# VectorE's background operations of a scan step, issued between the scan and its product

## The chip, the cores and the metric

The kernel runs on one core of a Trainium2 chip. The metric is the device time of one execution in microseconds. A core has five engines that run their own instruction queues in order: TensorE (PE in the profile; PEld is its weight loads), VectorE (DVE), ScalarE (ACT), GpSimd (POOL) and SyncE (SP, which issues the DMAs here). They wait for each other through semaphores.

## The reference

Eight images of 64 x 64 x 96 pass through two residual layers. The first, which fills nearly all of the time, is a two-dimensional state space layer: group norm, an input projection, a depthwise 3 x 3 convolution with SiLU, then a scan over the 4096 pixels in four directions, a layer norm, a gate and an output projection. The second is a group norm followed by an MLP on a twice upsampled image. The scan, for each of 4 directions, 192 channels and 16 states:

```python
def step(h, inp):
    ul, dl, Bl, Cl = inp
    dA = jnp.exp(dl[..., None] * A)
    h = dA * h + (dl * ul)[..., None] * Bl[:, :, None, :]
    y = jnp.einsum('bkdn,bkn->bkd', h, Cl)
    return (h, y)
```

## The kernel before

The 128 partitions of a scan tile are 8 channels by 16 states; its free dimension is a chunk of 1024 pixels. An image takes 4 directions x 4 chunks x 24 tiles, so 8 images make 3072 tiles, one step of the main loop each (`for i in range(n + 4)`). All instructions are issued in an order written out by hand; each engine runs its own in that order. For a tile there are:

- `fetch` (L1063), six steps ahead: a DMA that broadcasts delta * u (`du`) to the tile `dub`.
- `product_b` (L1069), three steps ahead: GpSimd multiplies `dub` by `br` into `bb`, one of four buffers.
- `decay` (L1075, L1082), one step ahead: four TensorE matmuls spread delta over the partitions into `pd` in PSUM, which has two buffers, and ScalarE takes the exponential in place.
- `scan` (L1089): VectorE's scan along the chunk, from `pd` and `bb`, started from the tile's column of `carry`. In steps with `i % 3 == 2` (`by_pool`) it writes to a tile `h` of its own, in the others back into `pd`.
- `product_c` (L1095): the product of the states by C (`cr`) into `hc`, on VectorE; for a `by_pool` tile on GpSimd, in the next step.
- `hold` (L1108): the last column of the states is copied to `carry`, on VectorE, for a `by_pool` tile on ScalarE. The last chunk of a direction has none.
- `sums` (L1127): TensorE adds `hc` over the states into `py`, for two tiles in every other step.

The scan's `pd` is thus read by the product and by the copy of the carry, in two of three steps, and the same buffer is written by the decay of the tile two steps later.

All else, that is the norms, projections, convolutions, gates and the MLP of other images and the deltas of the next chunk, is background work. It is written as generators that `Side` keeps in lists. One call of `side.advance` in each step lets the generators issue their next pieces, within caps on what a step may take of each engine. VectorE's pieces are few: `dl` (L1028), the convolution's and the gate's product (L585, L628), the statistics (L471, L481) and the layer norm's two products (L719, L720). The other engines' pieces are issued by the same call. A piece usually comes a step after the pieces of other engines that it reads. After `side.advance`, `turn_over` puts in a filler matmul (L1101) where the step had little for TensorE.

Of the kernel before, what the change touches and what calls it, by code (L numbers as in the profile page):

```python
# [136 lines left out]
def kernel(ctx: ExitStack, tc: tile.TileContext, a: dict, out: bass.AP):  # L137
# [133 lines left out]
    def constants_in():  # L271
        nc.gpsimd.memset(xp, 0.0)
        raw["sel"] = tile_([128, 8, 128], "sel_0")
        for hf in range(2):
            nc.sync.dma_start(
                raw["sel"][64 * hf : 64 * hf + 64].rearrange("p j m -> p (j m)"),
                a["sel_b"][0:64, 0:2].rearrange("r q j m -> r (q j m)"),
            )
        raw["dt_b"] = tile_([C, K, HF], "dt_b")
        nc.sync.dma_start(raw["dt_b"], a["dt_b"])  # L280
        names = ("xp_dt", "xp_c", "xp_b")
        raw["xp"] = [tile_([128, K, Q3, R if n == "xp_dt" else NS], n) for n in names]
        ds = raw["ds"] = tile_([128, Q3, K], "ds")
        for hf in range(2):
            for q, r0, r1, f, c0 in pieces:
                rows, src = slice(64 * hf + r0, 64 * hf + r1), slice(c0, c0 + r1 - r0)
                for t, name in zip(raw["xp"], names):
                    nc.sync.dma_start(t[rows, :, q, :], a[name][src, :, f, 0 : t.shape[-1]])
                nc.sync.dma_start(ds[rows, q, :], a["ds"][src, f, :])
        for name, shape in (("coef", [128, 3, 3]), ("w2", [128, 3, C]), ("b2", [128, C])):  # L290
            raw[name] = tile_(shape, name)
            nc.sync.dma_start(raw[name], a[name])
# [766 lines left out]
    def fetch(t):  # L1059
        assert t["got"]["ready"]  # L1060
        t["dub"] = sp.tile([128, T], F32, tag="dub", name="dub", bufs=4)
        g = t["g"]
        nc.sync.dma_start(  # L1063
            t["dub"], t["got"]["du"][None, 8 * g : 8 * g + 8, :].to_broadcast([NS, 8, T])
        )

    def product_b(t):
        t["bb"] = sp.tile([128, T], F32, tag="bb", name="bb", bufs=4)
        nc.gpsimd.tensor_tensor(t["bb"], t["dub"], t["got"]["br"], ALU.mult)  # L1069

    def decay(t):
        pd = t["pd"] = psd.tile([128, T], F32, tag="pd", name="pd")
        for hf in range(2):
            rows = slice(64 * hf, 64 * hf + 64)
            nc.tensor.matmul(  # L1075
                pd[:, MB * hf : MB * hf + MB],
                sel_b[rows, 4 * t["s"] + t["j"]].rearrange("p n c -> p (n c)"),
                t["got"]["dl"][rows, t["q"], :],
                start=True,
                stop=True,  # L1080
            )
        nc.scalar.activation(pd, pd, AF.Exp, scale=neg_a[:, t["k"], t["g"] : t["g"] + 1])  # L1082
# [10 lines left out]
    def product_c(t):  # L1093
        t["hc"] = sp.tile([128, T], F32, tag="hc", name="hc", bufs=4)
        (nc.gpsimd if t["by_pool"] else nc.vector).tensor_tensor(t["hc"], t["h"], t["got"]["cr"], ALU.mult)  # L1095

    def turn_over():

        if side.spent < 1.0 and side.free:
            n, p = side.bank("idle")  # L1100
            nc.tensor.matmul(p, ident, sel_b[:, 0:4].rearrange("p j n c -> p (j n c)"), start=True, stop=True)  # L1101
            side.give(n)

    def hold(t):
        if t["last"]:
            return
        end = T - 1 if t["k"] < 2 else 0
        (nc.scalar.copy if t["by_pool"] else nc.vector.tensor_copy)(  # L1108
            carry[:, t["g"] : t["g"] + 1], t["h"][:, end : end + 1]
        )  # L1110
# [61 lines left out]
    with tc.manual_schedule():  # L1172
        side.queue = [bp.open("setup")]
        side.drain()
        constants_in()
        start, rest = front(0)
        side.queue = start[:-4]
        side.drain()
        side.queue = start[-4:] + [(8, 0, constants_of_scans), (8, 0, constants_of_mlp)]
        side.drain()  # L1180
        side.urgent = prepare(0, tiles[0]["k"], tiles[0]["i0"], tiles[0]["got"])
        side.queue, rest = rest[:4], rest[4:]
        while side.urgent or side.hurried:
            side.advance({e: (2 * most, 2 * most) for e, (_, most) in Side.CAPS.items()}, 2, 0)
        n = len(tiles)
        for i in range(FETCH):
            fetch(tiles[i])
            if i >= FETCH - LEAD:
                product_b(tiles[i - FETCH + LEAD])
        decay(tiles[0])  # L1190
        begin, *side.later = prepare(0, tiles[NT]["k"], tiles[NT]["i0"], tiles[NT]["got"])
        total = 1
        for i in range(n + 4):
            t = tiles[i] if i < n else None
            at = i % (NT * NCH * K)
            if t and t["i"] == 0:
                b = t["b"]
                if at == 0:
                    y_dram[b] = [dr.tile([DI, L], F32, tag=f"y{o}", name=f"y{o}") for o in range(2)]
                    side.begun, hasty = 0, sum(item[1] for item in rest) if b == 0 else 0  # L1200
                    side.queue += rest
                    down, end = [], []
                    if b:
                        keep = {}
                        side.queue += tail(b - 1, keep)
                        up, down, end = mlp(b - 1, keep)
                        side.queue += up
                    if b + 1 < images:
                        start, rest = front(b + 1)
                        side.queue += start[:2] + [i for two in zip(down, start[2:10]) for i in two] if b else start[:10]  # L1210
                        side.queue += start[10:] + rest
                        rest = []
                    else:
                        side.queue += down
                    side.queue += end
                    total = sum(item[1] for item in side.queue)
                if b == images - 1 and at == NT * NCH * (K - 1):
                    keep = {}
                    side.queue += tail(b, keep, pairs=False)
                    total = 0  # L1220

            ahead = 4 if i < 2 * NT else 8
            if (i + ahead) % NT == 0 and i + ahead + NT < n:
                nxt = tiles[i + ahead + NT]
                begin, *side.later = prepare(nxt["b"], nxt["k"], nxt["i0"], nxt["got"])
                side.urgent.append(begin)

            if i == 2:
                side.urgent.append(begin)
            if i == 4 or i and i % NT == 0:  # L1230
                side.urgent += side.later
                side.later = []
            if t and t["i"] % 8 == 4:
                before(t)
            if i + FETCH < n:
                fetch(tiles[i + FETCH])
            if 0 < i <= n and tiles[i - 1]["by_pool"]:
                product_c(tiles[i - 1])
            if i + LEAD < n:
                product_b(tiles[i + LEAD])  # L1240
            if i + 1 < n:
                decay(tiles[i + 1])
            if t:
                scan(t)
                if not t["by_pool"]:
                    product_c(t)
                hold(t)
            ends = i % 2 == 1 and 3 <= i <= n + 2
            adds = ends and tiles[i - 2]["j"] == 3 and tiles[i - 2]["k"]
            side.advance(  # L1250
                Side.CAPS,
                2 if not total or side.begun < max(hasty, total * at / 290) else 0,
                0 if 7 <= i % NT <= 21 else 1,
                0.95 * (bool(ends) + bool(adds)),
            )
            turn_over()
            if ends:
                sums(tiles[i - 3 : i - 1])
                if tiles[i - 2]["j"] == 3:
                    side.stores.append([g := store(tiles[i - 2]), next(g)])  # L1260
        up, down, end = mlp(images - 1, keep)
        side.queue += up + down + end
        side.drain()
# [89 lines left out]
```

## Time and profile before

| | |
|---|---|
| median of 3 runs | 11111.8 us (11110.65 to 11118.07) |
| profiled execution, first to last instruction (its span) | 11105.8 us |
| the same execution's other time | none recorded; the span is 6.0 us under the median |
| VectorE busy, instructions | 10207.5 us, 7702 |
| GpSimd busy | 10179.6 us |
| TensorE busy | 9967.9 us, 932.0 of it filler (L1101) |
| ScalarE busy | 5910.6 us |
| mean granted TensorE clock | 0.982 |
| one scan on VectorE | 2.28 to 2.35 us, 3072 of them |
| one product on VectorE | 1225 ns, 2048 of them |
| one copy of the carry on VectorE | 148 ns, 1536 of them |

The busy shares tell how full an engine is over the whole span, not which engine sets the end. The list of waits has the waiting engine and line, the releaser, the time in total, the number of waits and the longest. A wait for several semaphores is put down to the one that came last. A row of the timeline has the start and the duration in us, engine, line, operation, the tiles (out<-in) and shapes, and in brackets the idle time of the engine before it with its releaser.

### The profile page before, as it was taken

Reading aid. Unit: us, or ns where it says so; the run is one execution under the profiler, and the core shown is the slowest. Engines: PE = TensorE matmul, PEld = TensorE weight load, DVE = VectorE, ACT = ScalarE, POOL = GpSimd, SP = SyncE. Lnnn points to the kernel's source line nnn. Section 1 sums busy time; section 2 is a strip of 40 time slices with the busy share of each in tenths; the row PEclk is TensorE's granted clock in tenths of the full one; section 3 lists DMA queues with packets and bytes.
Section 4 is the critical chain, followed back from the end, with each engine's and each line's share of the span. In section 5 each row is a group of like instructions: output and inputs, shape, how many; then the busy total and the mean of one; then the engine's idle time right before and its main releaser. Section 6 shows DMA issues by size and latency. Waiting matters only on the chain. (4 is left out here: it accounts for less than half of the span.)

```text
span 11105.8 us, 137238 instructions
## 1 busy us (share of the span) xinstructions
PE 9967.9 (90%) x45020; PEld 3204.6 (29%) x45020; DVE 10207.5 (92%) x7702; ACT 5910.6 (53%) x8218; POOL 10179.6 (92%) x4674
## 2 busy tenths in 40 slices
PE   8898888989889998999889998899988989889988
PEld 2222222322233222332223322233222332223325
DVE  6999999999999999999999999999999999999990
ACT  5455445656455564555545555455554655545543
POOL 5999999999999999999999999999999999999990
PEclk9999999999999999999999999999999999999998
DMA  6888898898988989888988989889898898988981
GB/s 174 215 208 224 209 231 209 217 227 232 233 209 216 225 231 225 212 218 224 240 217 215 224 221 244 209 219 225 217 243 210 217 228 218 247 206 216 227 214 48
DMA packets 1044463, 2401.27 MB, mean 216 GB/s; under 512 B 293820, under 2 KB 314556, under 8 KB 1043752
## 3 DMA queue, kind: packets, MB, share of 16 engines
q1 hardware_dynamic: 1042776, 2391.45, 86.5%
q8 instruction: 361, 5.91, 0.2%
q14 instruction: 350, 2.87, 0.1%
q10 hardware_dynamic: 976, 1.04, 0.0%
HBM read 1929.05 MB, written 328.73 MB: 203 GB/s over the span
## 5 line engine op out<-in xcount | busy, mean ns | idle before, releaser
L1069 POOL TENSOR_TENSOR bb<-dub,br 128x1024 f32<-128x1024 f32 x3072 | 7173.5, 2359 | 208.4 <-DMA dub<-du 149.2
L1082 ACT ACTIVATE pd<-pd,neg_a 128x1024 f32<-128x1024 f32 x3072 | 3340.7, 1088 | 4533.0 <-PE pd L1075 4489.8
L1075 PE MATMUL pd<-dl,sel_b 64*128 64x512 f32 x12288 | 3512.7, 645 | 987.2 <-DVE carry L1108 649.2
L1089 DVE TENSOR_TENSOR_SCAN pd<-pd,carry,bb 128x1024 f32<-128x1024 f32 x1536 | 3610.3, 2350 | 262.2 <-ACT carry L1108 127.9
L1095 POOL TENSOR_TENSOR hc<-h,cr 128x1024 f32<-128x1024 f32 x1024 | 2413.9, 2357 | 352.6 <-DVE h L1089 300.7
L1095 DVE TENSOR_TENSOR hc<-pd,cr 128x1024 f32<-128x1024 f32 x2048 | 2508.4, 1225 | 164.1 <-PE py L1127 20.0
L1075 PEld LDWEIGHTS pd<-dl,sel_b 64*128 64x128 f32 x12288 | 966.7, 186 | 3266.3 <-issue 1511.2
L1089 DVE TENSOR_TENSOR_SCAN h<-pd,carry,bb 128x1024 f32<-128x1024 f32 x768 | 1797.3, 2340 | 5.8 <-ACT pd L1082 5.6
L1127 PE MATMUL py<-hc,sel_r 128*32 128x512 f32 x12288 | 1715.0, 617 | 30.4 <-POOL hc L1095 30.2
L1089 DVE TENSOR_TENSOR_SCAN pd<-pd,bb 128x1024 f32<-128x1024 f32 x512 | 1172.5, 2290 | 98.6 <-ACT carry L1108 75.3
L1101 PE MATMUL idle<-sel_b,ident 128*128 128x512 f32 x1652 | 932.0, 646 | 8.0 <-DVE ty L720 5.9
L562 PE MATMUL pc<-pad,convr 96*128 96x512 f32 (+1 forms) x2304 | 858.3, 616 | 5.7 <-DVE e L585 3.6
L1089 DVE TENSOR_TENSOR_SCAN h<-pd,bb 128x1024 f32<-128x1024 f32 x256 | 583.6, 2280 | 26.0 <-ACT pd L1082 25.2
L1127 PEld LDWEIGHTS py<-hc,sel_r 128*32 128x32 f32 x12288 | 250.3, 109 | 1109.0 <-issue 854.5
L1031 POOL TENSOR_TENSOR u<-dl,u 128x512 f32<-128x512 f32 x384 | 485.0, 1271 | 79.2 <-DVE dl L1028 79.2
L862 PEld LDWEIGHTS p<-w2q,mq 128*100 128x100 f32 x4800 | 452.9, 168 | 274.6 <-issue 214.2
L855 PE MATMUL ph<-xu,w 96*128 96x500 f32 x960 | 504.9, 629 | 11.5 <-ACT mq L856 6.7
L862 PE MATMUL p<-w2q,mq 128*100 128x96 f32 x4800 | 511.5, 258 | 2.3 <-ACT mq L856 2.3
L562 PEld LDWEIGHTS pc<-pad,convr 96*128 96x128 f32 (+1 forms) x2304 | 266.3, 163 | 563.9 <-issue 552.8
L987 PE MATMUL px<-u,xp 64*64 64x512 f32 x1536 | 422.4, 627 | 2.4 <-issue 2.4
L1101 PEld LDWEIGHTS idle<-sel_b,ident 128*128 128x128 f32 x1652 | 249.8, 189 | 596.5 <-issue 522.4
L1012 PE MATMUL pv<-xd,dt_w 64*64 64x512 f32 x1536 | 394.4, 609 | 1.0 <-ACT xd L997 1.0
(153 smaller groups left out, 6707.9 us busy)
## 6 DMA issues: line engine op xcount, KB each, us to landing
dub<-du SPq DMA_DIRECT2D x3072, 512.0 KB
u<-u SPq DMA_DIRECT2D x256, 384.0 KB
du<-u SPq DMA_DIRECT2D x768, 128.0 KB
y<-yq SPq DMA_DIRECT2D x768, 128.0 KB
br<-xd SPq DMA_DIRECT2D x256, 256.0 KB
cr<-xd SPq DMA_DIRECT2D x256, 256.0 KB
yp<-y SPq DMA_DIRECT2D x384, 128.0 KB
yp<-u SPq DMA_DIRECT2D x192, 128.0 KB
```

The source lines that it names most:

```text
L562: nc.tensor.matmul(t[rows].rearrange("p (i j) -> p i j", i=8), weights[:, cs], v["pad"][:, 8 * blk + kw : 8 * blk + kw + 8, kh : kh + H], ...
L855: nc.tensor.matmul(t[:, :px], w1[:, m, :], xu, start=True, stop=True)
L862: nc.tensor.matmul(t[:SIDE, C * i : C * i + C], sq[:, m, row], w2q[:, m, :], start=(m == 0), stop=(m == 2))
L987: nc.tensor.matmul(p[rows], xp[rows, k, q, :], v["u"][rows, q, :], start=(q == 0), stop=(q == 2), skip_group_check=True,)
L1031: nc.gpsimd.tensor_tensor(v["u"][:, q, :], got["dl"][:, q, :], v["u"][:, q, :], ALU.mult)
L1069: nc.gpsimd.tensor_tensor(t["bb"], t["dub"], t["got"]["br"], ALU.mult)
L1075: nc.tensor.matmul(pd[:, MB * hf : MB * hf + MB], sel_b[rows, 4 * t["s"] + t["j"]].rearrange("p n c -> p (n c)"), t["got"]["dl"][rows, t[" ...
L1082: nc.scalar.activation(pd, pd, AF.Exp, scale=neg_a[:, t["k"], t["g"] : t["g"] + 1])
L1089: nc.vector.tensor_tensor_scan(t["h"][:, ::step], pd[:, ::step], t["bb"][:, ::step], 0.0 if t["first"] else held, ALU.mult, ALU.add)
L1095: (nc.gpsimd if t["by_pool"] else nc.vector).tensor_tensor(t["hc"], t["h"], t["got"]["cr"], ALU.mult)
L1101: nc.tensor.matmul(p, ident, sel_b[:, 0:4].rearrange("p j n c -> p (j n c)"), start=True, stop=True)
L1127: nc.tensor.matmul(py[r0 : r0 + 32], sel_r[:, t["j"], :], t["hc"][:, MB * hf : MB * hf + MB], start=(t["j"] == 0), stop=(t["j"] == 3 and t ...
```

## The change

In the steps whose product is VectorE's, the product by C and the copy of the carry are issued after the call of `side.advance` instead of ahead of it. VectorE's order in such a step was scan, product, copy, background; it becomes scan, background, product, copy. In the `by_pool` steps the order stays: scan, ScalarE's copy, background.

```diff
             if t:
                 scan(t)
-                if not t["by_pool"]:
-                    product_c(t)
-                hold(t)
+                if t["by_pool"]:
+                    hold(t)
             ends = i % 2 == 1 and 3 <= i <= n + 2
             adds = ends and tiles[i - 2]["j"] == 3 and tiles[i - 2]["k"]
             side.advance(
...
                 0.95 * (bool(ends) + bool(adds)),
             )
+            if t and not t["by_pool"]:
+                product_c(t)
+                hold(t)
             turn_over()
             if ends:
                 sums(tiles[i - 3 : i - 1])
```

## Prediction

> **What bounds the kernel now.** I read the busy shares first, then who waits for whom on VectorE, then single rows in order of time.
>
> From the profile page, part 1:
>
> ```profile
> PE 9967.9 (90%) x45020; PEld 3204.6 (29%) x45020; DVE 10207.5 (92%) x7702; ACT 5910.6 (53%) x8218; POOL 10179.6 (92%) x4674
> ```
>
> Three engines stand at 90% or more. The busy time by stretches says that the scans run from 120 to 10835 us; in these 10715 us VectorE is busy for 10162 us and GpSimd for 10150 us, 95% each. Which of them leads is told by the waits. VectorE's waits, the longest three:
>
> ```profile
> DVE pd L1089 <- ACT carry L1108: 203.2, 414, 3.6
> DVE pd L1089 <- ACT pd L1082: 113.8, 238, 8.0
> DVE pd L1089 <- POOL bb L1069: 40.2, 38, 2.3
> ```
>
> VectorE's scan waits for ScalarE (the exponential of the decay, or the copy queued beside it: 317 us) and hardly for GpSimd (40 us). GpSimd in turn waits 301 us for VectorE's `h`. So VectorE leads, and the wait that ends last in front of its scans is the decay's.
>
> Steps go in threes. I call them A, B (product on VectorE) and C (`by_pool`, product on GpSimd). Going through the trace's 3072 scans in order, the idle time in front of A's scan is 324 us, of B's 37, of C's 32. A group of three, from the timeline (only its VectorE, decay and exponential rows):
>
> ```profile
> 3351.92 2.35 DVE L1089 TENSOR_TENSOR_SCAN pd<-pd,carry,bb 128x1024 f32<-128x1024 f32 x1
> ...
> 3354.37 1.23 DVE L1095 TENSOR_TENSOR hc<-pd,cr 128x1024 f32<-128x1024 f32 x1
> 3355.51 0.15 DVE L1108 COPY carry<-pd 128x1 f32<-128x1 f32 x1
> 3355.57 2.34 DVE L1089 TENSOR_TENSOR_SCAN h<-pd,carry,bb 128x1024 f32<-128x1024 f32 x1
> 3355.77 0.33 PEld L1075 LDWEIGHTS pd<-dl,sel_b 64*128 64x128 f32 x4 [1.41 <-PE ph L855]
> 3355.80 1.13 PE L1075 MATMUL pd<-dl,sel_b 64*128 64x512 f32 x4 [0.63 <-DVE carry L1108]
> 3356.97 1.09 ACT L1082 ACTIVATE pd<-pd,neg_a 128x1024 f32<-128x1024 f32 x1 [1.08 <-PE pd L1075]
> 3358.16 2.36 DVE L1089 TENSOR_TENSOR_SCAN pd<-pd,carry,bb 128x1024 f32<-128x1024 f32 x1 [0.25 <-ACT carry L1108]
> ```
>
> Rows one to three are step B, row four is C, the last is the next A. There are two `pd` buffers, so A's decay may start only when B's copy of the carry, the last reader of that buffer, is over (3355.66). From there: 0.11 to the weight load and 1.16 to the matmuls' end, 0.04 to the exponential, 1.09 in it, 0.10 to the scan: 2.50 us. Beside it VectorE has only C's scan, over at 3357.91, so it idles 0.25. Next to a scan that waits for nothing (which starts 0.08 before its forerunner's recorded end) this is 0.33 us lost.
>
> The same place where step B has a background operation (VectorE alone):
>
> ```profile
> 2806.43 1.23 DVE L1095 TENSOR_TENSOR hc<-pd,cr 128x1024 f32<-128x1024 f32 x1
> 2807.57 0.15 DVE L1108 COPY carry<-pd 128x1 f32<-128x1 f32 x1
> 2807.63 0.68 DVE L1028 SCALAR_TENSOR_TENSOR dl<-pv,e 128x512 f32<-128x512 f32 x1
> 2808.23 2.28 DVE L1089 TENSOR_TENSOR_SCAN h<-pd,bb 128x1024 f32<-128x1024 f32 x1
> 2810.43 2.27 DVE L1089 TENSOR_TENSOR_SCAN pd<-pd,bb 128x1024 f32<-128x1024 f32 x1
> ```
>
> Here `dl` fills the time and A's scan follows without idling.
>
> **What the change moves.** Only two VectorE instructions of steps A and B, the product and the copy of the carry, go behind `side.advance`. Neither issues a DMA, and no order changes on TensorE, ScalarE, GpSimd or SP; what changes there is when their waits on VectorE end. Nothing happens in a step without background work. By count over the trace, such work stands in 190 A steps, 222 B steps and 294 C steps; C keeps its order.
>
> **Gain: the distance between scan and product.** Over 2048 pairs the product starts 0.080 us after the scan's end on average (half at 0.035, half at 0.105; above, 3351.92 + 2.35 = 3354.27, then 3354.37). Pairs in which the second doesn't read what the first wrote overlap by 0.084 (product to copy, copy to background, background to scan). One background pair that does depend, L719 to L720, is 0.035 apart as well. So the distance belongs to the dependence. With a background operation between, both distances become -0.084: 0.164 us saved per step, 412 x 0.164 = 67.6 us.
>
> [...]
>
> **Cost 1: the decay of the next A.** In B the copy of the carry now follows the background work, so the 2.50 us begin 0.60 - 0.16 = 0.43 later (a lone operation of 0.68 takes 0.60 with its overlap), and the cover is C's scan alone. In 66 of the 222 groups C has background work too; it takes 0.6 or more, over the 0.33 needed: nothing is lost. In the other 156, 119 did not wait before and now lose 0.33 each: 39.3 us. By hand: -67.6 + 39.3 = -28.
>
> **Cost 2: where TensorE is behind anyway.** In a quarter of the groups with work in B the decay's weight load came 0.5 us or more after the copy: TensorE was busy with background matmuls, A's scan waited for it, and VectorE's gain vanishes in that wait. So I took group by group the later of two times, VectorE free (0.164 earlier per moved step) and the exponential's end (later by what the copy is later), carrying a late copy of A through TensorE's idle time to the next A. If TensorE's lateness swallows that of the copy, the sum over 1021 groups is -6 us; if it swallows nothing, +30 us:
>
> ```
> background in   groups   0.164s   lateness swallows   swallows nothing
> B                   90    -12.2          +8.4               +29.2
> B, C                48     -6.7         -13.4                -0.2
> A                   65    -11.0          -2.4                -2.4
> A, C                40     -6.9          -2.2                -2.2
> A, B                66    -20.0         +11.2               +12.1
> A, B, C             18     -5.5          -5.5                -5.5
> none or C          694      0            -1.7                -0.6
> ```
>
> **Cost 3: waits that now stand before the product.** A background operation that waits holds up the product, the copy and, through it, the decay. Its inputs' ends against its scan's end: `dl` (L1028) ready at least 0.97 us before, L585 0.67, L628 0.76. Only `bn_stats` (L471, 7.3 us in all) and L719 (1.1 us) would wait: +8 us. Below nothing this cannot be, since an operation issued earlier waits no less.
>
> **Covered.** A's late copy delays C's decay, whose exponential ended at least 1.13 us before C's scan in the groups with work in A; one operation moves it 0.43: 0. The products come later for TensorE's sums, which read them one to three steps later: 0. Background outputs come up to 1.3 us sooner; in the trace ScalarE and TensorE wait some 25 us each for `dl`, not on VectorE's path: 0, at best a few us.
>
> **Sum.** -6 + 8 = +2 to +30 + 8 = +38. I take the middle, +20, because both kinds of groups (TensorE waiting, TensorE late) are common. The profiled execution lasts 11105.8 from first to last instruction, 6.0 under the median of the runs, so 11105.8 + 20 + 6 = 11132 us. A measurement of this kernel can tell about 0.2%, 22 us, from no change; this is just inside.
>
> **Rivals.**
> *Slower by TensorE's backlog.* TensorE is released 0.43 to 1.2 us later (0.56 on average) in up to 412 steps. Where its idle time before the next decay is shorter, the delay goes on to side matmuls, ScalarE's side work and the next exponential, also that of B's scan. It decides where that idle time is under 0.56 us: by the 190 groups with work in A (quartiles 0.19, 0.83, 1.12) a little over a third. 412 x 0.56 / 3 = 77, with the -6 about +70: 11182 us. Against it: 932 us of TensorE's time are filler matmuls (L1101). 0.22.
> *Faster.* All 67.6 us come, and the decay is not exposed because a TensorE that gets its background results sooner is less behind: 11044 us. Against it: the clean group above, where 2.50 stands against 2.25 whatever TensorE does. 0.14.
> *The distance is the product's own*, not the dependence's, so it stays: the 67.6 are gone, -6 + 68 = +62: 11174 us. Against it: L719 to L720. For it: no row shows a product anywhere but behind its scan. 0.12.
>
> **How the numbers follow.** The forecast's case gets 0.52: its own range, -32 (the hand sum and some waits of products on TensorE that are covered) to +38, lies mostly within 0.2%: 0.36 same, 0.14 slower, 0.02 faster. Backlog: 0.19 slower, 0.03 same. Faster: 0.13 and 0.01 same. Own distance: 0.08 slower, 0.03 same, 0.01 faster. Together faster 0.16, same 0.43, slower 0.41. The range goes from the forecast's low end (11105.8 - 32 + 6 = 11080) to the backlog's price, 11182; it leaves out most of the faster case and the far part of the backlog.
>
> **What would show it.** Right: products behind background work start 0.08 before its end; idle time in front of A's scan rises by 40 to 70 us from 324, that of B and C stays under 50; VectorE's busy sum stays while its overlaps grow. Wrong: products still 0.03 to 0.10 late (the third rival); B's idle time well up, with TensorE as releaser (backlog); A's idle time unchanged (faster).

## The result, and the profile after

The changed kernel takes 11148.55 us (median of 6 runs, 11145.35 to 11175.53) against 11114.93 us for the kernel before beside it: 1.0035 times as long, 95% interval 1.0023 to 1.0047. By this ratio it is 39 us slower (the two medians lie 34 us apart), clear of the 0.2% that the prediction named.

The profiled execution lasts 11144.8 us from first to last instruction, 39.0 more than before. Page, part 1, the engines' line:

```profile
PE 9999.2 (90%) x45020; PEld 3208.9 (29%) x45020; DVE 10177.3 (91%) x7702; ACT 5903.1 (53%) x8218; POOL 10181.4 (91%) x4674
```

VectorE has the same 7702 instructions, 30 us less busy time and a longer span: its instructions overlap more, and it idles more. VectorE's waits (waiting line, releaser: total us, times, longest):

```profile
DVE pd L1089 <- ACT carry L1108: 238.9, 468, 3.9
DVE pd L1089 <- ACT pd L1082: 165.1, 350, 8.0
DVE h L1089 <- ACT pd L1082: 51.6, 22, 5.9
...
DVE pd L1089 <- POOL bb L1069: 26.5, 28, 2.3
```

The scans' waits for ScalarE grew by 36 and 51 us on their two `pd` lines, the C scans (`h`) wait 52 us where it was 31; GpSimd holds up the scans for 27 us, less than before. Adding up VectorE's rows step by step gives the whole difference:

```
VectorE                          before    after   change, us
busy (overlaps counted once)    10207.5  10177.3    -30.2
idle before products              164.1    118.7    -45.4
idle before A's scans             324.2    385.3    +61.2
idle before B's scans              36.6     49.0    +12.5
idle before C's scans              31.8     51.8    +20.1
idle before background work        28.5     49.1    +20.5
sum                                                 +38.7
```

The first two lines are the gain, 75.6 us; the other four the cost, 114.3.

**The gain and the first cost** are seen in one group, the counterpart of the one shown before (timeline, VectorE's rows and the exponential that A waits for):

```profile
2809.93 2.29 DVE L1089 TENSOR_TENSOR_SCAN pd<-pd,bb 128x1024 f32<-128x1024 f32 x1
...
2812.12 0.67 DVE L1028 SCALAR_TENSOR_TENSOR dl<-pv,e 128x512 f32<-128x512 f32 x1
2812.72 1.21 DVE L1095 TENSOR_TENSOR hc<-pd,cr 128x1024 f32<-128x1024 f32 x1
2813.84 0.15 DVE L1108 COPY carry<-pd 128x1 f32<-128x1 f32 x1
2813.91 2.28 DVE L1089 TENSOR_TENSOR_SCAN h<-pd,bb 128x1024 f32<-128x1024 f32 x1
...
2815.31 1.09 ACT L1082 ACTIVATE pd<-pd,neg_a 128x1024 f32<-128x1024 f32 x1 [2.89 <-PE pd L1075]
...
2816.50 2.30 DVE L1089 TENSOR_TENSOR_SCAN pd<-pd,bb 128x1024 f32<-128x1024 f32 x1 [0.31 <-ACT carry L1108]
```

`dl` starts 0.10 before the scan's recorded end and the product 0.07 before `dl`'s: both distances overlap, as worked out. From scan to scan, B now takes 3.98 us; it took 3.52 + 0.60 = 4.12 (2804.11 to 2808.23). But the copy ends later, the decay with it, and A's scan idles 0.31 where before it followed at once.

**The cost that the prediction hadn't seen.** In the seventh image a group has two deltas in A and one in C. Its own three scans stand 30.0 to 30.2 us behind those of the kernel before, the next group's first scan 33.3: some 3.1 us are lost in between. TensorE and VectorE there, before:

```profile
9268.97 0.15 DVE L1108 COPY carry<-pd 128x1 f32<-128x1 f32 x1
9269.04 1.28 DVE L1028 SCALAR_TENSOR_TENSOR dl<-pv,e 128x512 f32<-128x512 f32 x2
9269.18 1.13 PE L1075 MATMUL pd<-dl,sel_b 64*128 64x512 f32 x4 [1.31 <-DVE carry L1108]
...
9270.24 1.98 PE L562 MATMUL pc<-pad,convr 96*128 96x512 f32 x4
...
9272.15 1.06 PE L1127 MATMUL py<-hc,sel_r 128*32 128x512 f32 x8
```

And after:

```profile
9297.85 1.27 DVE L1028 SCALAR_TENSOR_TENSOR dl<-pv,e 128x512 f32<-128x512 f32 x2
...
9300.16 0.15 DVE L1108 COPY carry<-pd 128x1 f32<-128x1 f32 x1
...
9300.37 1.46 PE L1075 MATMUL pd<-dl,sel_b 64*128 64x512 f32 x4 [1.91 <-DVE carry L1108]
...
9301.75 3.78 PE L562 MATMUL pc<-pad,convr 96*128 96x512 f32 x4
...
9305.46 1.94 PE L1127 MATMUL py<-hc,sel_r 128*32 128x512 f32 x8
...
9309.95 2.36 DVE L1089 TENSOR_TENSOR_SCAN pd<-pd,carry,bb 128x1024 f32<-128x1024 f32 x1 [3.21 <-ACT carry L1108]
```

TensorE waits 1.91 us for the copy instead of 1.31, and then the same four matmuls take 3.78 instead of 1.98 us and the same eight 1.94 instead of 1.06. The next decay is late and VectorE idles 3.21 us. The busy times by stretches (length, then TensorE's and the other engines' busy time, then the granted clock) name the reason; first the stretch behind this wait in after, then the same one in before:

```profile
9300.30:9309.00 8.70, 8.63 (x21) 2.48 (x22) 6.41 (x6) 1.87 (x3) 8.49 (x5) 0.61 0.87 282
```

```profile
9269.10:9278.00 8.90, 7.98 (x28) 2.44 (x28) 8.87 (x9) 3.94 (x6) 8.90 (x6) 1.00 0.99 272
```

The granted clock is 0.61 in the mean of the stretch that follows the longer wait, and 1.00 before. The clock records of the two traces hold only 1.0 and 0.5, each for a whole multiple of 3.41 us; the one behind this wait holds 0.5 for 6.83 us, from 9301.05 on. Among the scans (from 100 us after the first to the last) TensorE ran at half clock in 62 stretches, 303.8 us, before, and in 81, 423.2 us, after.

Laying the two traces side by side group by group (three steps; the instructions are the same) tells the two costs apart. "Near" is a group that has a half-clock stretch in it or in the group just before or after it, in either trace:

```
background in   groups  forecast, us     measured   away from half clock        near
B                   90   +8.4 to +29.2     +24.5     45 groups, mean +0.170    +16.8
B, C                48  -13.4 to -0.2      -16.4     16        mean -0.145     -14.1
A                   66   -2.4               -4.9     55        mean -0.094      +0.3
A, C                40   -2.2              +23.3     16        mean -0.207     +26.7
A, B                66  +11.2 to +12.1     +21.6     24        mean -0.059     +23.1
A, B, C             18   -5.5               -6.6      4        mean -0.337      -5.3
none or C          695   -1.7 to -0.6       -2.8    541   sum -7.6              +4.9
all               1023   -5.6 to +30.4     +38.7    701   sum -13.6            +52.2
```

Where TensorE keeps its clock the change is a gain, of 13.6 us here and of 4.6 in the second trace of the changed kernel that is named below; the loss is all in the 322 groups near half clock. Which part of those 52 us is the clock's own doing and which the groups' other waits, this table can't say. That there are other waits shows in the lone-B groups: 13.6 of their 16.8 us come from one place in each image, the step with the aggregated statistics (L481). In the seventh image after:

```profile
8610.28 0.58 ACT L810 COPY t1s<-p 100x512 f32<-100x512 f32 x1 [7.05 <-DMA t<-t1s]
...
8612.81 2.29 DVE L1089 TENSOR_TENSOR_SCAN h<-pd,bb 128x1024 f32<-128x1024 f32 x1 [5.64 <-ACT pd L1082]
```

ScalarE's copy waits for a DMA, the exponential stands queued behind it, and the half clock comes only afterwards (from 8611.55). In the kernel before the copy waits 2.98 us and the scan 1.37. Two groups earlier the changed kernel gets 10.7 us back, and the A only kernel below has the same pair (+9.7 and -8.9), so most of this seems to be a wait that changed its place; no run was made to tell why. The experiments go on to the clock.

### The profile page after: what moved, and what is told of

It reads as the page before. It is cut to its first block, busy times and chain, and to the rows that moved or that the text cites. A ratio compares the mean times of both kernels' runs of the same rounds, so it can differ in the third digit from the quotient of the medians.

```text
span 11144.8 us, 137182 instructions
## 1 busy us (share of the span) xinstructions
PE 9999.2 (90%) x45020; PEld 3208.9 (29%) x45020; DVE 10177.3 (91%) x7702; ACT 5903.1 (53%) x8218; POOL 10181.4 (91%) x4674
```

## The experiments

Theories: *the exposed decay* (theory 1: A's decay behind a late copy of B, and nothing else), *the clock* (theory 2: longer waits of TensorE bring half clock) and *the backlog* (late copies push TensorE's queue back at full clock; the prediction's rival). "Half" is half-clock time among the scans of the one profiled execution; the ratio is against the kernel before on the same chip, with its 95% interval.

**A steps only, B steps only.** The condition on `by_pool` in the change becomes one on the step's number; the other steps keep the old order:

```diff
-            if t and not t["by_pool"]:
+            if t and t["i"] % 3 == 0:    # B only: == 1
                 product_c(t)
                 hold(t)
```

> Only the A steps (i % 3 == 0) have the background work before the product; B steps are as before. Theory 1 (the loss is the exposed decay of the next A after a late copy of B; the gain is 0.164 us per moved step): the gain of 190 steps, 31 us, stays and nothing is exposed: 25 to 31 us faster than before (0.22 to 0.28%), idle time in front of A's scan 320 to 330 us as before. Theory 2 (a good part of the loss is TensorE's clock: its longer idle times in moved steps bring half-clock stretches, 304 us of them among the scans before, 423 after): A steps bring such stretches too (groups with work in A and C lost 23 us in the changed kernel), so half-clock time 340 to 380 us and between 15 us faster and no change.

Measured: 1.0019 (1.0010 to 1.0027), 21 us slower; half 386 us. Theory 1 alone is finished: no decay of A was to stand exposed, yet 31 us of gain became a loss, and idle time before A's scans is 388 us, not 320 to 330. The 714 groups away from half clock gained 13.0 us, those near lost 55.1 (this profiled execution lies 10 us over its kernel's median). The clock theory had the sign of the extra half clock, but neither its amount nor the size of the loss.

> Only the B steps (i % 3 == 1) have the background work before the product; A steps are as before. Theory 1: all of the loss is here: gain 222 x 0.164 = 36, exposed decay 51 to 61, waits of the moved statistics 18: 35 to 45 us slower than before, idle time in front of A's scan 375 to 385 us. Theory 2: the loss is shared between both kinds of step: 15 to 30 us slower, half-clock time among the scans 340 to 400 us.

Measured: 1.0029 (1.0019 to 1.0040), 32 us slower; half 389 us; idle time before A's scans 352 us, not 375. Between the two forecasts. Lone-B groups away from half clock lose 0.158 each, nearly as in the changed kernel. The two halves cost more alone (21 + 32) than together (39): the losses don't add up.

**A filler in the moved steps.** `turn_over` puts its filler matmul also where VectorE had background work in an A or B step and a PSUM bank is free. That gave 118 fillers more, for 412 such steps (one filler leaves two rows in the trace: 1888 rows, where there were 1652); in the changed kernel and, as a control, in the kernel before:

```diff
-            turn_over()
+            turn_over(t and not t["by_pool"] and side.vec > 0)
...
-        if side.spent < 1.0 and side.free:
+        if (side.spent < 1.0 or late) and side.free:
```

> The changed kernel, with TensorE's filler matmul also put into every A or B step that issues background work of VectorE, so that TensorE is idle for less of the wait for the late copy. Theory 1: the copy is as late as before the filler, so the time stays at 30 to 40 us over the kernel before, or grows by what the filler delays. Theory 2: half-clock time among the scans falls from 423 to 320 or less, and the time falls to 10 to 20 us over the kernel before.

Measured: 1.0074 (1.0062 to 1.0086), 82 us slower; half 324 us.

> The kernel before with the same filler matmuls: the control. Theory 1: no change (within 10 us), the filler only fills idle time. Theory 2: half-clock time among the scans falls a little from 304 us, to 240 to 290, and the time falls by 5 to 15 us, less than the filler brings in the changed kernel.

Measured: 1.0028 (1.0017 to 1.0039), 31 us slower; half 280 us. In both the half-clock time fell about as the clock theory says, and the time rose, which is a miss for it. These fillers cost more than the clock gives back: of the groups with work in A alone, away from half clock, the 39 that got a filler lose 0.48 us each in the control and the other 22 nothing, most likely because the filler still runs when the next decay could start. Half-clock time alone doesn't set the time.

**Only the first background operation before the product.** The product and the copy follow VectorE's first background operation, between the two of a layer norm pair too; the rest comes after. A last `side.slip()` behind `side.advance`, left out here as are other lines, serves the steps without background work:

```diff
+    def slip(self):
+        if self.waiting:
+            go, self.waiting = self.waiting, None
+            go()
...
             entry[1] = next(entry[0], None)
+            if need.get("dve"):
+                self.slip()
...
+                if t["i"] % 3 in (0, 1):    # second kernel: (0,)
+                    def finish(t=t):
+                        product_c(t)
+                        hold(t)
+                    side.waiting = finish
```

> In A and B steps only the first background operation of VectorE goes between the scan and the product; product and copy follow, then the rest (between the two of a layer norm pair, too). Every moved step keeps its gain (412 x 0.164 = 68 us), the copy is late by 0.43 us at most instead of up to 1.2. Clock theory (the loss comes from half-clock stretches that follow a window of 3.4 us in which TensorE was less than half busy; steps with two operations make most of the new ones): half-clock time among the scans falls from 423 to 350 us or less, time 15 us faster to 10 us slower than before. Backlog theory (a late copy only pushes TensorE's queue back, at full clock): the delay falls by about a third, 15 to 25 us slower than before, whatever the half-clock time.

Measured: 0.9990 (0.9981 to 0.9999), 11 us faster; half 345 us. The clock theory's numbers hold, the backlog's do not. Of the 50 us to the changed kernel some 11 are another gain: in 90 layer norm pairs the product now fills the distance between the two operations too (90 x 0.119).

> The same in A steps alone; B steps as before. Gain 190 x 0.164 = 31 us and no decay of A exposed. Clock theory: half-clock time as before, 280 to 330 us, and 15 to 30 us faster than before. Backlog theory: the A only kernel lost 20 us; with copies late by 0.43 instead of 0.56 on average it still loses 5 to 15 us.

Measured: 0.9977 (0.9968 to 0.9986), median 11093.17 us, 26 us faster than before; half 276 us, just under the 280 to 330 forecast. This is the fastest of all kernels here. Against the A only kernel (1.0019) the one difference is what happens in A steps with two operations, 57 of them, and that is worth 47 us, about 0.8 us a step (4 to 5 us of it the distance inside 38 layer norm pairs, which the product now fills too). VectorE in such a step:

```profile
9243.99 2.33 DVE L1098 TENSOR_TENSOR_SCAN pd<-pd,carry,bb 128x1024 f32<-128x1024 f32 x1
9246.23 0.67 DVE L1037 SCALAR_TENSOR_TENSOR dl<-pv,e 128x512 f32<-128x512 f32 x1
9246.82 1.21 DVE L1104 TENSOR_TENSOR hc<-pd,cr 128x1024 f32<-128x1024 f32 x1
9247.95 0.15 DVE L1117 COPY carry<-pd 128x1 f32<-128x1 f32 x1
9248.02 0.68 DVE L1037 SCALAR_TENSOR_TENSOR dl<-pv,e 128x512 f32<-128x512 f32 x1
9248.61 2.35 DVE L1098 TENSOR_TENSOR_SCAN pd<-pd,carry,bb 128x1024 f32<-128x1024 f32 x1
```

Everything overlaps, and the copy is late by one operation. It is the step where TensorE waited 1.91 us in the changed kernel.

**The filler in steps with two operations.** As above with `side.vec > 1.2`:

> The changed kernel with the filler matmul of TensorE added only in A and B steps with two background operations (111 steps), where TensorE's wait for the copy is the longest. Clock theory: half-clock time falls from 423 to 340 us or less and the time by 10 to 25 us, to 10 to 25 us over the kernel before. Backlog theory: a filler adds to TensorE's queue, so the time stays or grows: 35 to 50 us over the kernel before.

Measured: 1.0037 (1.0025 to 1.0050); half 423 us. Inconclusive: the filler needs a free PSUM bank, and the trace has 18 filler rows more than the changed kernel's 1652, so 9 fillers came into being, of 111.

**The copy alone late.** The product stays behind the scan; only the copy goes behind `side.advance`:

```diff
                 if t["by_pool"]:
                     hold(t)
+                else:
+                    product_c(t)
...
-                product_c(t)
                 hold(t)
```

> In A and B steps the product stays right behind the scan and only the copy of the carry goes behind the background work: the late copy without the gain (the scan's distance to its product stays, and the copy is later by the whole 0.60 us of an operation instead of 0.43). Both theories: the changed kernel's loss and the 68 us that are not gained: 90 to 130 us slower than before (0.8 to 1.2%). If the product's distance had nothing to do with the order, it would be 35 to 50 us slower, like the changed kernel. Clock theory: half-clock time 420 us or more.

Measured: 1.0054 (1.0042 to 1.0067), 60 us slower; half 406 us. Both theories missed the time, and the half-clock time is under the 420 forecast. It is slower than the changed kernel, so the move of the product is a gain, but only of some 21 us by the ratios (34 by the two traces) and not of 68. Away from half clock the price of a step is near what was worked out (groups with work in A: +0.095 against -0.094; in A and C: +0.026 against -0.207). Near half clock the sums differ little (+48.8 against +52.2): there the saved distance seems to become a longer wait for TensorE.

**A filler that fits into the wait.** In steps with two operations the filler goes to the bank that the background work has just given back, so it needs no free one (110 fillers came into being):

```diff
+        if late and side.given:
+            p = side.again(side.given[-1], "idle")
+            nc.tensor.matmul(p, ident, sel_b[:, 0:4].rearrange("p j n c -> p (j n c)"), start=True, stop=True)
-        if side.spent < 1.0 and side.free:
+        elif side.spent < 1.0 and side.free:
```

> The changed kernel with a filler matmul in the A and B steps with two background operations, written to the PSUM bank that the step's background work has just given back, so that it needs no free bank (the earlier try found a free one in only 18 steps) and runs while TensorE waits for the late copy. Clock theory: half-clock time among the scans falls from 423 to 360 us or less and the time by 10 to 25 us although TensorE has more to do: 10 to 25 us over the kernel before. Backlog theory: more work on TensorE, the time stays or grows: 35 us or more over the kernel before.

(The 18 steps named there were 18 rows, nine fillers.) Measured: 1.0062 (1.0048 to 1.0076), 69 us slower; half 403 us. As a whole a miss for the clock theory. By groups it falls apart: against the changed kernel, those with work in A and C take 29.5 us less, at one place in four images 3.24 to 3.29 us less each, and no half clock follows there any more. Those with work in A and B take 37 us more, those in B and C 22: in a layer norm pair the bank is given back only after the pair's second operation. The fillers waited 218 us for it in all (10 in the changed kernel), the sums queued behind them, and in nine groups that lose 2.3 us each half clock now follows where there was none.

**The same in the 21 steps without layer norm pairs.**

```diff
-            turn_over(t and not t["by_pool"] and side.vec > 1.2)
+            turn_over(t and not t["by_pool"] and side.vec > 1.2 and not side.norm)
```

> The changed kernel with a filler matmul in only the 21 A and B steps that have two background operations which are no layer norm pair, into the bank that the first of them has given back, so that it runs in TensorE's wait for the copy. (In the layer norm pairs the filler of the try before had to wait for the pair's last operation and came too late.) Clock theory: 21 matmuls more, and the group of the half-clock stretch that follows each of these steps gets some 3 us of its time back at the places seen in the try before (29 us in the groups with work in A and C): 20 to 35 us faster than the changed kernel, 0 to 15 us over the kernel before, half-clock time among the scans 320 to 375 us. Backlog theory: no faster than the changed kernel, 30 to 42 us over the kernel before.

Measured: 1.0014 (1.0003 to 1.0025), 16 us over the kernel before; the changed kernel had 1.0035 and, once more, 1.0034. So some 22 us come back (about 16 either way, estimated from the three intervals), that is from more work on TensorE; the time missed its forecast (0 to 15) by a hair. The trace has 20 fillers, not 21: the step with two statistics just misses the condition. The groups with work in A and C account for the gain: 29.6 us less than in one trace of the changed kernel, 30.7 less than in the other. Nearly all of it lies in the 18 of them that have two operations in A. In each trace of the changed kernel 16 of these hold a half-clock stretch; with the fillers one does. At the place shown above:

```profile
9306.00 1.27 DVE L1032 SCALAR_TENSOR_TENSOR dl<-pv,e 128x512 f32<-128x512 f32 x2
...
9307.32 1.12 PE L1105 MATMUL idle<-sel_b,ident 128*128 128x512 f32 x2 [0.71 <-DVE dl L1032]
9308.31 0.15 DVE L1115 COPY carry<-pd 128x1 f32<-128x1 f32 x1
...
9308.52 1.13 PE L1079 MATMUL pd<-dl,sel_b 64*128 64x512 f32 x4
9309.58 1.98 PE L565 MATMUL pc<-pad,convr 96*128 96x512 f32 x4
...
9314.85 2.36 DVE L1093 TENSOR_TENSOR_SCAN pd<-pd,carry,bb 128x1024 f32<-128x1024 f32 x1
```

The copy is as late as in the changed kernel (2.31 us from the deltas' start to the copy's, in both). The filler, which waits for the second of the two deltas, splits TensorE's wait; the four matmuls take 1.98 us again, and A's scan doesn't wait. That is the clock shown by itself; the backlog theory has the opposite sign here. What did not come as forecast is the total of half-clock time, 406 us where 320 to 375 was expected: this profiled execution was 20 us over its kernel's median, and other groups lost more in it than in the first trace of the changed kernel (lone B 12 us, A and B 15).

**No filler at all in the kernel before.** `side.spent < 1.0` becomes `side.spent < 0.0`:

> The kernel before without any of its 1652 filler matmuls (932 us of TensorE's busy time): what half-clock time costs, in the kernel before. Clock theory: half-clock time among the scans at least doubles (600 us or more) and the time grows by 50 us or more, some 0.2 to 0.5 us for each us at half clock. Backlog theory: TensorE's queue gets shorter, the time stays or falls by up to 20 us.

Measured: 1.0105 (1.0092 to 1.0119), 117 us slower; half 1331 us, mean granted clock 0.937. (The 1652 named there are rows, 826 fillers.) TensorE has 932 us less to do and the kernel is slower: the clock theory's sign. The price is 117 us for 1027 us more at half clock, 0.11 us each, less than the 0.2 forecast, probably because many of these stretches fall where TensorE has slack.

**The changed kernel again.**

> The changed kernel itself, beside the others on one chip. Both theories: 30 to 42 us slower than before, half-clock time among the scans 400 to 440 us.

Measured: 1.0034 (1.0021 to 1.0046), half 406 us, as expected. Most of its groups repeat: A and C +24.5, lone B +22.6. A and B has +32.1 where +21.6 was, all away from half clock -4.6 where -13.6 was.

## Why the prediction was right or wrong

The measured time lies in the range (11080 to 11182), but the likeliest case, no change within 0.2%, did not happen; the one with 0.41 did, slower. The forecast was +20 us, the runs say +39. That this is the upper end of the forecast's own sum (+38) is chance: groups with work in A and C and in A and B cost 35 us more than their rows in it, and the other rows came out 27 us under that end. Of the signs named, the products' overlap and the idle time before A's scans (+61, 40 to 70 forecast) came as forecast; B's and C's idle time ended at 49 and 52 us, at the limit of 50.

*The gain* (67.6 us) came to 75.6 on VectorE's own rows. The distance belongs to the dependence: products behind background work start 0.08 before its end. The third rival is out. But as time the gain is worth only some 21 to 34 us (the kernel with the copy alone late, against the changed one). The term was right in VectorE's idle time and two to three times too large in the kernel's.

*Cost 1*, A's decay exposed after work in B, is right in the mean: a lone-B group away from half clock loses 0.170 us (0.33 - 0.164 = 0.166), one with C's cover gains 0.145 (0.164). Single lone-B groups lie between -0.10 and +0.25, so the agreement to a hundredth is partly luck.

*Cost 2*, TensorE behind anyway: the sum by groups gave -6 to +30. B with C, and groups with work in all three steps, came out within 3 us of their rows. Lone B's 24.5 lies inside its row by luck: 13.6 of it are the wait behind ScalarE's copy at L481, which no term names (14.5 of 22.6 in the second trace). The step that failed is "carrying a late copy of A through TensorE's idle time". It took idle time for a cushion. In groups with work in A and C that gave -2.2 where +23.3 was measured, in A and B 12 where 22 was. Idle time had a price itself: the wait of 1.91 us shown above left TensorE busy for 44% of a window of 3.41 us, the clock record behind it holds 0.5, and the same four matmuls took 3.78 us for 1.98 (the last section counts such windows).

*Cost 3*, inputs not ready: 8 us forecast; idle time before background work rose by 20.5. 18.0 of it (13.8 in the second trace) is one place in six images, the first statistics (L471) of the next image. In the changed kernel's fifth image:

```profile
6398.98 2.35 DVE L1089 TENSOR_TENSOR_SCAN pd<-pd,carry,bb 128x1024 f32<-128x1024 f32 x1
...
6402.68 1.06 PE L465 MATMUL pt<-ident,x 128*96 128x128 f32 x4 [5.78 <-DMA x<-in_x]
...
6404.45 0.69 DVE L471 BATCH_NORM_STATS2 st<-pt 96x6 f32<-96x512 f32 x1 [3.12 <-ACT pad L469]
```

TensorE's transposes wait for the load of x, the statistics for ScalarE's copy of their result, and the product, which used to be ahead, now stands behind them. The term was seen, but taken from one execution; at this place the transposes waited 2.55 us for the load there and 5.78 here.

*Covered at 0* held where it was claimed: in the groups with work in A, idle time before C's scans did not rise. C's 20.1 us lie in lone-B groups, 15.8 of them at the L481 place in four images and 4.5 at the first statistics; neither wait was in the sum. B's 12.5 us belong to one execution (2.6 in the second trace).

*The backlog rival* named the right engine and had the mechanism upside down. It was to decide where TensorE's idle time is too short; the loss sits where it is too long, and giving TensorE more to do there won time back. The 20 fillers show this for the places with two operations in A and work in C: 29 to 31 us by the traces, some 22 by the times, against which stand the gains elsewhere. For the layer norm groups the clock is argued from the half-clock stretches beside them, but no filler could be fitted there: what part of their 22 to 32 us it is, stays open.

## What to carry to other kernels

Moving independent work between a producer and its consumer hides the dependence's latency (here 0.164 us a step), but it also delays every release that the consumer would have given: look at who waits for that release and what the wait does to that engine's clock (here TensorE waited 1.91 us instead of 1.31, with a granted clock of 0.61 instead of 1.00 behind it). Take the smallest piece that covers the latency, one operation, and only where the release has slack; that turned a loss of 0.35% into a gain of 0.23%. Before calling TensorE's idle time free, look at the granted clock behind it.

## What the runs showed of the hardware

The clock records of the two traces, of the kernel before and of the changed kernel, are 1.0 or 0.5, each for a whole multiple of 3.413 us. Cut into windows of that length, and taking all among the scans that ran at full clock, both traces together: of 106 with TensorE busy for less than 45%, the next window ran at half clock after 105; of 59 between 45 and 50%, after 29; of 71 between 50 and 55%, after 9; of 5783 above that, after none. The wait of 1.91 us shown above left a window that was 44% busy, and half clock followed; the wait of 1.31 us at the same place in the kernel before lies in a window that was 63% busy, and the clock stayed at 1.0. In the second trace of the changed kernel the same wait of 1.91 us in the sixth image is spread over two windows, 97% and 57% busy: no half clock follows and the group gains 0.14 us, where five other images lose 1.5 to 3.2. The windows' edges lie at another point against the first instruction in each of these two traces, 0.71 us (before) and 3.14 us (after) past a multiple of 3.413 us.
